# Columns of a gather table, two per VectorE operation

## The chip, the cores and the metric

The kernel runs on one core of a Trainium2 chip. The metric is the device time of one execution in microseconds (us). The engines in the text are PE (TensorE, with its weight loads as PEld), DVE (VectorE), ACT (ScalarE), POOL (GpSimd) and SP (SyncE), which here only issues DMAs.

## The reference

One layer of a graph network in float32. There are 12,500 nodes with 48 features, 400,000 edges with 32 features, and a hidden width of 128. The edges are sorted by destination.

```python
h = jnp.maximum(_layernorm(x, axis=-1), 0.0)
x_i, x_j = h[dst], h[src]
hid = relu(concatenate([x_i, x_j, edge_attr], axis=1) @ W1 + b1)
msg = hid @ W2 + b2
out = x + segment_sum(msg, dst, num_segments=12500)
```

The product with W1 can be parted: one part depends on the destination node, one on the source node and one on the edge. So two tables over the nodes hold the first two parts, and W2 is applied after the sum over the edges of a node.

## The kernel before, in words

A first stage (up to 67 us) computes the layer norm and builds two tables in DRAM with one row of 128 values per node: `tab_a` (the destination's part, with b1) and `tab_b` (the source's part).

The second stage, `windows`, goes over the edges in 391 chunks of 1024 edges, 8 tiles of 128. Since the edges are sorted, the destinations of a chunk lie in a window of `W` = 80 nodes, so a small one-hot matrix can stand for the gather by destination and for the sum. The source rows are in no order. They are the work that the change is about, and reach PE's sum in three ways:

- **gathers**: POOL issues one indirect DMA per tile (L358), which brings 128 rows of `tab_b` into the buffer `gb`. It has six buffers.
- **rows**: SP issues 12 DMAs of single rows per chunk (`rows`, L292); 128 of them, from several chunks, make a tile `gs` that replaces one gather. 36 tiles are made so.
- **columns**: the first 13 chunks (`BUILD`) also load `tab_b` and transpose it into SBUF, into `bt` (128 x 12,500: one column per node). From then on DVE and ACT copy single columns out of `bt` by an address in a register into a tile `gt` (`columns`, L339). PE transposes the tile and adds it to `pre` (`turned`, L394). `PARTS` says which columns of each chunk are whose: DVE 27 and 17, ACT 28 and 32. These 104 columns per chunk (`PART`) make 305 tiles that need no gather. The list `BYCOLS` names the chunk of each tile. 377 chunks copy columns.

The addresses stand in a table `last`; `load` (L274) brings the numbers of one part from it into an engine's registers with one instruction (TENSOR_LOAD).

The order on every engine is written out by hand (`tc.manual_schedule()`). In iteration c of the loop:

1. `prepare(c)`: SP loads the window's rows of `tab_a` (`rhs`, L347), the edge features (`lhs`, L349) and the destinations (`row`, L351). POOL issues the gathers of chunk c: eight, less one if the chunk has a tile of columns and one if it has a tile of rows. DVE compares the destinations with the window's first node (L366, one-hot in `lhs`, its sum in `deg`), loads the numbers of part 1, and makes the transposed one-hot `hot` (L372).
2. DVE's columns of parts 0 and 1.
3. PE: `before(c-1)` (L384, one-hot and edge features times `rhs` into `pre`), `fold(c-2)` (L416 and L419, the sum over the edges into `p_g`), `turned(c-1)` (L394).
4. ACT's columns of part 2; then `hidden(c-1)`: DVE adds `pre` and `gb` (L403, and L405 for a tile of rows), ACT applies the relu (L407 for a tile of columns, L408 for the rest).
5. ACT's columns of part 3; `add(c-2)`: DVE adds `p_g` to the window's place in a running buffer `seg` (L426). Every 12 chunks a finished segment of 1024 nodes is multiplied by W2, added to x and stored (L452 to L458), and the running buffer is changed (L442 to L444).
6. The numbers of parts 0 and 2 of chunk c+1 are loaded.

POOL's gathers of a chunk wait for a free `gb`, which `hidden` of an earlier chunk gives back. POOL also clears the three `deg` tiles (L251) at the start of `windows`.

Of the kernel before, what the change touches and what calls it, by code (L numbers as in the profile page):

```python
# [8 lines left out]
F32 = mybir.dt.float32  # L9
I32 = mybir.dt.int32  # L10
AF = mybir.ActivationFunctionType
ALU = mybir.AluOpType
# [4 lines left out]
P = 128  # L17
N, D, DE, HID, E = 12500, 48, 32, 128, 400000
# [6 lines left out]
NCH = (NT + T - 1) // T  # L25
W = 80
# [4 lines left out]
L = 1024  # L31
FAR = L - W
# [11 lines left out]
U8 = mybir.dt.uint8  # L44
# [5 lines left out]
COLS = BUILD + 1  # L50
ROWS0 = 3
END = NT // T

PARTS = ((True, 0, 27, 1), (True, 27, 17, 28), (False, 44, 28, 48), (False, 72, 32, 76))
PART = sum(n for _, _, n, _ in PARTS)
BASE = 108
RPART = 12

BT0 = 16512


SEG, NEXT, SEG2 = 122, 123, 124
WIDTH = 128
SLOTS = (NCH + 2 + P - 1) // P
MOST = 32

# [137 lines left out]
def windows(nc, tc, gp, bt, ident, idx, x_t, tab_a, tab_b, dst, edge_t, w1, w2s, b2s, out_t):  # L204


    srci, rel, bw, wrow, last = idx
    with ExitStack() as es:
        one = es.enter_context(tc.tile_pool(name="wone", bufs=1))
        ld = es.enter_context(tc.tile_pool(name="ld", bufs=3))  # L210
        gtp = es.enter_context(tc.tile_pool(name="gtp", bufs=3))
# [5 lines left out]
        ps_w = es.enter_context(tc.tile_pool(name="ps_w", bufs=1, space=PSUM))  # L217


        wnum = ps_w.tile([P, W], F32, name="wnum")  # L220
        nc.vector.tensor_scalar_add(wnum, wrow, -HALF)


        bt8 = bt.bitcast(U8)
        for _, _, n, at in PARTS:
            nc.vector.tensor_scalar(
                last[:, :, at : at + n], last[:, :, at : at + n], 4, BT0,
                op0=ALU.mult, op1=ALU.add,
            )
        rows_at = slice(BASE + 1, BASE + 1 + RPART)  # L230
# [3 lines left out]
        tab8 = tab_b.rearrange("n h -> (n h)").bitcast(U8)  # L234
# [8 lines left out]
        segs = []  # L243
        for k in range(2):
            seg = one.tile([P, 2, L], F32, name=f"seg{k}")
            nc.vector.memset(seg, 0.0)
            segs.append(seg)
        degs = []
        for k in range(3):
            deg = one.tile([W, P], F32, name=f"deg{k}")  # L250
            nc.gpsimd.memset(deg, 0.0)  # L251
            degs.append(deg)

        rhss = []
        for k in range(3):
            rhs = one.tile([P, HID], F32, name=f"rhs{k}")
            nc.sync.dma_start(rhs[W:K, :], w1[2 * D :, :])
            rhss.append(rhs)
        st = {}
        gts = {}  # L260
        gss = {}

        def group(c):

            return divmod(c + OFF, GQ)
# [15 lines left out]
        def node(n):  # L281
            return n.with_bounds(min_val=0, max_val=N - 1)
# [32 lines left out]
        regs = {}  # L315

        def load(c, part):

            dve, first, n, at = PARTS[part]
            n = max(0, min(n, len(BYCOLS) * P - ((c - COLS) * PART + first))) if c >= COLS else 0  # L320
            engine = mybir.EngineType.DVE if dve else mybir.EngineType.Activation
            if part == 0 and 2 <= c < NCH + 2:
                base, *nodes = numbers(c, at - 1, n + 1, engine)
                st[c - 2]["base"] = base.with_bounds(min_val=0, max_val=FAR)
            else:
                nodes = numbers(c, at, n, engine) if n else []
            regs[c, part] = nodes

        def columns(c, part):

            dve, first, _, _ = PARTS[part]
            copy = nc.vector.tensor_copy if dve else nc.scalar.copy
            for k, at in enumerate(regs.pop((c, part), [])):
                j, e = divmod((c - COLS) * PART + first + k, P)
                of = BYCOLS[j]
                if of not in gts:
                    gts[of] = gtp.tile([HID, P], F32, name="gt")
                at = at.with_bounds(min_val=BT0, max_val=BT0 + 4 * (N - 1)) - BT0
                copy(gts[of].bitcast(U8)[:, 4 * e : 4 * e + 4], bt8[:, bass.ds(at, 4)])  # L339

        def prepare(c):
            n = min(T, NT - c * T)
            at = c * CE
            m = max(0, min(RPART, len(BYROWS) * P - (c - ROWS0) * RPART)) if c >= ROWS0 else 0
            base, *nodes = numbers(c, BASE, 1 + m, mybir.EngineType.SP)
            rhs = rhss[c % 3]
            nc.sync.dma_start(rhs[:W, :], tab_a[bass.ds(node(base), W), :])  # L347
            lhs = ld.tile([P, CE], F32, name="lhs")
            nc.sync.dma_start(lhs[W:K, : n * P], edge_t[:, at : at + n * P])  # L349
            row = ld.tile([W, CE], I16, name="row")  # L350
            nc.sync.dma_start(  # L351
                row[:, : n * P],
                dst[at : at + n * P].rearrange("(o e) -> o e", o=1).to_broadcast([W, n * P]),
            )
            st[c] = dict(n=n, rows=nodes)
            gb = gp.tile([P, T, HID], F32, name="gb")
            for t in range(n - (c in BYCOLS) - (c in BYROWS)):
                nc.gpsimd.indirect_dma_start(  # L358
                    out=gb[:, t, :], out_offset=None, in_=tab_b[:, :],
                    in_offset=bass.IndirectOffsetOnAxis(  # L360
                        ap=srci[:, c * T + t : c * T + t + 1], axis=0
                    ),
                )

            deg = degs[c % 3]
            nc.vector.tensor_scalar(  # L366
                lhs[:W, : n * P], row[:, : n * P], bw[:, c : c + 1], None,
                op0=ALU.is_equal, op1=ALU.add, accum_out=deg[:, :1],
            )
            load(c, 1)  # L370
            hot = wp.tile([P, T, W], F32, name="hot")
            nc.vector.tensor_tensor(  # L372
                hot[:, :n, :], wnum.unsqueeze(1).to_broadcast([P, n, W]),
                rel[:, c * T : c * T + n].unsqueeze(2).to_broadcast([P, n, W]), op=ALU.is_equal,
            )
            st[c].update(rhs=rhs, lhs=lhs, gb=gb, deg=deg, hot=hot)

        def before(c):
# [43 lines left out]
        def add(c):  # L422

            s = st.pop(c)
            to = segs[group(c)[0] % 2][:, :, bass.ds(s["base"], W)]
            nc.vector.tensor_add(to, to, s["p_g"])  # L426

        xs = {}
# [31 lines left out]
        with tc.manual_schedule():  # L460
            for c in range(NCH + 2):
                if c < NCH:
                    prepare(c)
                    if c < BUILD:
                        part = turn_load(c)
                    rows(c, st[c].pop("rows"))
                columns(c, 0)
                columns(c, 1)
                if 0 <= c - 1 < NCH:
                    before(c - 1)  # L470
                if 0 <= c - 2 < NCH:
# [157 lines left out]
def tile_gnn_preln(  # L629
# [129 lines left out]
    outside = nc.values_load(flag[:1, :1], min_val=0, max_val=1)  # L759

    with tc.If(outside == 0) as cmp:
        windows(nc, tc, gp, bt, ident, (srci, rel, bw, wrow, last), x_t, tab_a, tab_b, dst16, edge_t,
                w1, w2s, b2s, out_t)
    with cmp.Else():
        general(nc, tc, bt, ident, x_t, tab_a, tab_b, src_it, dst_it, dst, edge_t, w1, w2s, b2s,
# [71 lines left out]
```

## Time and profile before

| | |
|---|---|
| median of 3 runs | 4946.85 us (4942.31 to 4949.29) |
| the profiled execution | 4948.09 us, span 4946.4 us |
| granted PE clock, mean | 0.607 |
| instructions | 92158 |
| DMA | 363.63 MB, mean 74 GB/s |
| POOL idle before a gather, released by DVE's L426 | 1273.1 us in 337 times |

The span is the time from the first to the last instruction of the profiled execution; the time beside it has what lies around it. The busy shares are means over the whole span. The seven or eight gathers of a chunk are called a burst. A line such as `gt<-bt 128x4 uint8 x16540 | 1516.0, 193 | 1464.2 <-issue 1457.9` says: 16540 operations that write `gt` from `bt`, 1516.0 us busy in all, 193 ns each, 1464.2 us of idle time of the engine just before them, of which 1457.9 us ended with "issue" (the engine waited for nothing that the profile shows). Operations overlap, so 193 ns is the time from the start of one to its end, not the distance to the next.

### The profile page before, as it was taken

To read this page: it belongs to the slowest core of one execution; us is meant where nothing else is said; L and a number is where in the kernel's file an instruction comes from. 1 tells how busy PE (TensorE), PEld (TensorE's weight loads), DVE (VectorE), ACT (ScalarE), POOL (GpSimd) and SP (SyncE) were. 2 spreads that over 40 slices of the span, in tenths; PEclk is the share of its full clock that TensorE was granted. 3 is DMA by queue.
4 is the path that set the end of the run, shared out by engine and by line. 5 is a ranking of instruction groups with operands and counts; after the bars stand their busy time and mean duration, and the time that the engine had idled before them with its cause. 6 is when DMAs were issued, how large, how long until landed. Compare 5 with 4: busy or idle time off the path is not lost. (4 is left out here: it accounts for less than half of the span.)

```text
span 4946.4 us, 92158 instructions
## 1 busy us (share of the span) xinstructions
PE 3197.2 (65%) x14504; PEld 2884.0 (58%) x14504; DVE 2942.6 (59%) x18764; ACT 2864.2 (58%) x23270; POOL 2675.9 (54%) x2812
## 2 busy tenths in 40 slices
PE   4565666666666666666666666666666666666666
PEld 3555556555555555656555555655666555555656
DVE  3255666666666666566666666666566666666665
ACT  2146666666566666566656566666566666566665
POOL 5555555555555555555555555555555555555552
PEclk7665655566666565556565666555555665666555
DMA  5422222222222222222222222222222222222221
GB/s 208 111 78 71 70 70 67 68 70 72 70 70 68 67 70 71 70 70 69 66 70 71 70 70 68 67 70 70 70 70 68 68 69 71 70 69 69 70 67 51
DMA packets 214695, 363.63 MB, mean 74 GB/s; under 512 B 70419, under 2 KB 119717, under 8 KB 212805
## 3 DMA queue, kind: packets, MB, share of 16 engines
q0 software_dynamic: 89120, 182.66, 14.4%
q1 hardware_dynamic: 124704, 174.89, 11.8%
q14 instruction: 491, 4.01, 0.3%
q8 instruction: 120, 1.97, 0.2%
q10 hardware_dynamic: 260, 0.10, 0.0%
HBM read 337.91 MB, written 22.07 MB: 73 GB/s over the span
## 5 line engine op out<-in xcount | busy, mean ns | idle before, releaser
L358 POOL DMA_INDIRECT gb<-tab_b,srci x2784 | 2654.2, 953 | 2167.6 <-DVE seg L426 1273.1
L339 ACT COPY gt<-bt 128x4 uint8 x22500 | 2421.0, 189 | 1761.1 <-issue 1734.7
L339 DVE COPY gt<-bt 128x4 uint8 x16540 | 1516.0, 193 | 1464.2 <-issue 1457.9
L416 PE MATMUL p_g<-hot,hid 128*128 128x80 f32 x6250 | 1368.2, 407 | 1557.6 <-ACT hid L408 1446.3
L416 PEld LDWEIGHTS p_g<-hot,hid 128*128 128x128 f32 x6250 | 1291.5, 314 | 1648.2 <-ACT hid L408 1528.5
L384 PEld LDWEIGHTS pre<-rhs,lhs 112*128 112x128 f32 x6250 | 1254.8, 306 | 140.1 <-issue 95.7
L384 PE MATMUL pre<-rhs,lhs 112*128 112x128 f32 x6250 | 1291.4, 393 | 52.1 <-DVE hid L403 38.8
L366 DVE TENSOR_SCALAR_CACHE_REDUCE lhs<-row,bw 80x1024 f32<-80x1024 int16 x391 | 498.1, 1274 | 253.5 <-issue 181.1
L403 DVE TENSOR_TENSOR hid<-pre,gb 128x896 f32<-128x896 f32 (+2 forms) x391 | 429.7, 1099 | 67.5 <-remote 53.8
L408 ACT ACTIVATE hid<-hid 128x896 f32<-128x896 f32 (+1 forms) x391 | 376.1, 962 | 120.4 <-DVE hid L403 91.1
L372 DVE TENSOR_TENSOR hot<-wnum,rel 128x640 f32<-128x640 f32 x391 | 322.0, 823 | 95.7 <-issue 95.7
L394 PE MATMUL pre<-ident,gt 128*128 128x128 f32 x610 | 220.0, 464 | 93.6 <-remote 49.8
L419 PE MATMUL p_g<-ident,deg 80*128 80x80 f32 x782 | 237.4, 405 | 2.7 <-issue 2.7
L394 PEld LDWEIGHTS pre<-ident,gt 128*128 128x128 f32 x610 | 164.0, 328 | 101.3 <-remote 53.6
L419 PEld LDWEIGHTS p_g<-ident,deg 80*128 80x128 f32 x782 | 203.4, 317 | 2.7 <-issue 2.7
L426 DVE TENSOR_TENSOR seg<-seg,p_g 128x160 f32 x391 | 120.9, 309 | 51.3 <-issue 23.4
L452 PE MATMUL p_f<-seg,w2s 128*48 128x512 f32 (+1 forms) x134 | 121.9, 1010 | 0.4 <-DVE seg L426 0.4
L407 ACT ACTIVATE hid<-pre 128x128 f32<-128x128 f32 x305 | 81.9, 268 | 60.8 <-DVE hid L403 51.7
L453 PE MATMUL p_f<-seg,b2s 1*48 1x512 f32 (+1 forms) x134 | 111.2, 924 | 0.0
L453 PEld LDWEIGHTS p_f<-seg,b2s 1*48 1x48 f32 x134 | 14.5, 159 | 102.0 <-issue 102.0
L311 ACT COPY bt<-pre 128x1024 f32<-128x1024 f32 (+1 forms) x13 | 12.4, 957 | 94.7 <-remote 71.5
L454 DVE TENSOR_TENSOR xseg<-xseg,p_f 48x512 f32<-48x512 f32 (+1 forms) x67 | 45.0, 671 | 29.7 <-PE p_f L453 22.5
(65 smaller groups left out, 348.7 us busy)
## 6 DMA issues: line engine op xcount, KB each, us to landing
gs<-tab_b SPq DMA_DIRECT2D x4608, 0.5 KB
row<-in_dst SPq DMA_DIRECT2D x390, 160.0 KB
lhs<-in_edge_t SPq DMA_DIRECT2D x390, 128.0 KB
gb<-tab_b,srci POOLq DMA_INDIRECT x2784
rhs<-tab_a SPq DMA_DIRECT2D x391, 40.0 KB
xseg<-in_x_t SPq DMA_DIRECT2D x33, 192.0 KB
out_x<-xseg SPq DMA_DIRECT2D x33, 192.0 KB
hid<-tab_b SPq DMA_DIRECT2D x12, 512.0 KB
```

The lines of the kernel that those rows point to most:

```text
L339: copy(gts[of].bitcast(U8)[:, 4 * e : 4 * e + 4], bt8[:, bass.ds(at, 4)])
L358: nc.gpsimd.indirect_dma_start(out=gb[:, t, :], out_offset=None, in_=tab_b[:, :], in_offset=bass.IndirectOffsetOnAxis(ap=srci[:, c * T + t ...
L366: nc.vector.tensor_scalar(lhs[:W, : n * P], row[:, : n * P], bw[:, c : c + 1], None, op0=ALU.is_equal, op1=ALU.add, accum_out=deg[:, :1],)
L372: nc.vector.tensor_tensor(hot[:, :n, :], wnum.unsqueeze(1).to_broadcast([P, n, W]), rel[:, c * T : c * T + n].unsqueeze(2).to_broadcast([P ...
L384: nc.tensor.matmul(pre[:, t, :], s["lhs"][:K, t * P : (t + 1) * P], s["rhs"][:K, :], start=True, stop=c not in BYCOLS or t < n - 1,)
L394: nc.tensor.matmul(s["pre"][:, s["n"] - 1, :], gts.pop(c), ident, start=False, stop=True)
L403: nc.vector.tensor_add(h[:, :g, :], pre[:, :g, :], s["gb"][:, :g, :])
L408: nc.scalar.activation(h[:, :m, :], h[:, :m, :], AF.Relu)
L416: nc.tensor.matmul(p_g[:, 0, :], s["h"][:, t, :], s["hot"][:, t, :], start=t == 0, stop=t == n - 1)
L419: nc.tensor.matmul(p_g[:, 1, :], s["deg"], ident[:W, :W], start=True, stop=True)
L452: nc.tensor.matmul(p_f[:, :n], w2s, seg[:, 0, s], start=True, stop=False)
L453: nc.tensor.matmul(p_f[:, :n], b2s[:1, :], seg[:1, 1, s], start=False, stop=True)
```

## The change

- DVE no longer copies single columns. One `tensor_scalar` takes two: its input is a pair of words, all ones and zero (`first`, in PSUM beside `wnum`), its two scalars are two columns of `bt` at register addresses, and the two operations are AND and XOR on bits. The first word becomes colA XOR colB, the second colB. When a group of pairs is done, one `tensor_tensor` (`part_pairs`) XORs the second words into the first, and so leaves colA and colB.
- ACT copies one float32 instead of four bytes.
- DVE's columns come in three parts, 24, 18 and 12 (54 for 44), each loaded by an instruction of its own; ACT's stay 28 and 32 (60). `PART` becomes 114, so 334 tiles instead of 305 come from columns, and POOL issues 2755 gathers instead of 2784.
- On DVE, part 0 moves ahead of `hot`; its load for the next chunk comes straight after `hidden`, ahead of part 2's parting and of `add`.
- The place of `add` and the row address of `rhs` come out of the table `last` as byte addresses, without a register instruction for each; `seg` gets a pool of its own and `last` wider rows (136 for 128).
- The `deg` tiles are made and cleared ahead of the first stage.

In the new file the pair operation is L361, the parting L375, ACT's copy L368, POOL's gather L400, the one-hots L408 and L415, `hidden` L447, ACT's relu of the eight or seven tiles L451, `turned` L438 and `add` L475.

```diff
-PARTS = ((True, 0, 27, 1), (True, 27, 17, 28), (False, 44, 28, 48), (False, 72, 32, 76))
+PARTS = (
+    (True, 0, 24, 1), (True, 24, 18, 25), (True, 42, 12, 43),
+    (False, 54, 28, 56), (False, 82, 32, 84),
+)
...
+        segs = [seg.tile([P, 2, L], F32, name=f"seg{k}") for k in range(2)]
...
-        wnum = ps_w.tile([P, W], F32, name="wnum")
+        wmask = ps_w.tile([P, W + 2], F32, name="wnum")
+        wnum = wmask[:, :W]
         nc.vector.tensor_scalar_add(wnum, wrow, -HALF)
+
+        first = wmask[:, W:].bitcast(I32)
+        nc.vector.memset(first[:, :1], -1)
+        nc.vector.memset(first[:, 1:], 0)
...
             if part == 0 and 2 <= c < NCH + 2:
                 base, *nodes = numbers(c, at - 1, n + 1, engine)
-                st[c - 2]["base"] = base.with_bounds(min_val=0, max_val=FAR)
+                st[c - 2]["base"] = base
...
         def columns(c, part):
-            dve, first, _, _ = PARTS[part]
-            copy = nc.vector.tensor_copy if dve else nc.scalar.copy
-            for k, at in enumerate(regs.pop((c, part), [])):
-                j, e = divmod((c - COLS) * PART + first + k, P)
+            dve, first_of, _, _ = PARTS[part]
+            nodes = regs.pop((c, part), [])
+            step = 2 if dve else 1
+            runs = {}
+            for k in range(0, len(nodes), step):
+                j, e = divmod((c - COLS) * PART + first_of + k, P)
                 of = BYCOLS[j]
                 if of not in gts:
                     gts[of] = gtp.tile([HID, P], F32, name="gt")
-                at = at.with_bounds(min_val=BT0, max_val=BT0 + 4 * (N - 1)) - BT0
-                copy(gts[of].bitcast(U8)[:, 4 * e : 4 * e + 4], bt8[:, bass.ds(at, 4)])
+                if dve:
+                    nc.vector.tensor_scalar(
+                        gts[of].bitcast(I32)[:, e : e + 2], first,
+                        column(nodes[k]).bitcast(I32), column(nodes[k + 1]).bitcast(I32),
+                        op0=ALU.bitwise_and, op1=ALU.bitwise_xor,
+                    )
+                    runs.setdefault(of, [e, e])[1] = e + 2
+                else:
+                    nc.scalar.copy(gts[of][:, e : e + 1], column(nodes[k]).bitcast(F32))
+            odd[c, part] = [(gts[of], *run) for of, run in runs.items()]
+
+        def part_pairs(c, part):
+            for gt, e0, e1 in odd.pop((c, part), []):
+                two = gt.bitcast(I32)[:, e0:e1].rearrange("h (k t) -> h k t", t=2)
+                nc.vector.tensor_tensor(
+                    two[:, :, 0], two[:, :, 0], two[:, :, 1], op=ALU.bitwise_xor
+                )
...
         def prepare(c):
...
-            nc.sync.dma_start(rhs[:W, :], tab_a[bass.ds(node(base), W), :])
+            base = base.with_bounds(min_val=0, max_val=4 * HID * (N - 1))
+            nc.sync.dma_start(
+                rhs.bitcast(U8)[:W, :],
+                taba8[bass.ds(base, 4 * HID * W)].rearrange("(w h) -> w h", w=W),
+            )
...
             load(c, 1)
+            columns(c, 0)
             hot = wp.tile([P, T, W], F32, name="hot")
...
+            load(c, 2)
...
         def add(c):
-            to = segs[group(c)[0] % 2][:, :, bass.ds(s["base"], W)]
+            k = group(c)[0] % 2
+            of = SEG0 + k * SEG_SIZE
+            at = s["base"].with_bounds(
+                min_val=of, max_val=of + 4 * FAR, guaranteed_mod_val=0, out_of_modulus=4
+            ) - of
+            to = segs[k].bitcast(U8)[:, :, bass.ds(at, 4 * W)].bitcast(F32)
             nc.vector.tensor_add(to, to, s["p_g"])
...
-                columns(c, 0)
+                if c >= NCH:
+                    columns(c, 0)
                 columns(c, 1)
+                part_pairs(c, 0)
+                columns(c, 2)
+                part_pairs(c, 1)
...
-                columns(c, 2)
+                columns(c, 3)
                 if 0 <= c - 1 < NCH:
                     hidden(c - 1)
-                load(c, 3)
-                columns(c, 3)
+                load(c + 1, 0)
+                part_pairs(c, 2)
+                load(c, 4)
+                columns(c, 4)
                 if 0 <= c - 2 < NCH:
                     add(c - 2)
...
-                load(c + 1, 0)
-                load(c + 1, 2)
+                load(c + 1, 3)
...
+    degs = []
+    for k in range(3):
+        deg = const.tile([W, P], F32, name=f"deg{k}")
+        nc.gpsimd.memset(deg, 0.0)
+        degs.append(deg)
     gp = ctx.enter_context(tc.tile_pool(name="gp", bufs=6))
```

More of the change, by code (lines that the diff above doesn't have):

```diff
@@ L52 @@
 END = NT // T
-PARTS = ((True, 0, 27, 1), (True, 27, 17, 28), (False, 44, 28, 48), (False, 72, 32, 76))
+PARTS = (
+    (True, 0, 24, 1), (True, 24, 18, 25), (True, 42, 12, 43),
+    (False, 54, 28, 56), (False, 82, 32, 84),
+)
 PART = sum(n for _, _, n, _ in PARTS)
-BASE = 108
+BASE = 116
 RPART = 12
 BT0 = 16512
-SEG, NEXT, SEG2 = 122, 123, 124
-WIDTH = 128
+SEG0 = 123360
+SEG_SIZE = 8 * L
+SEG, NEXT, SEG2 = 130, 131, 132
+PLACE0 = 133
+WIDTH = 136
 SLOTS = (NCH + 2 + P - 1) // P
@@ L204, in windows @@
 def windows(nc, tc, gp, bt, ident, idx, x_t, tab_a, tab_b, dst, edge_t, w1, w2s, b2s, out_t):
-    srci, rel, bw, wrow, last = idx
+    srci, rel, bw, wrow, last, degs = idx
     with ExitStack() as es:
+        seg = es.enter_context(tc.tile_pool(name="segs", bufs=1))
+        segs = [seg.tile([P, 2, L], F32, name=f"seg{k}") for k in range(2)]
         one = es.enter_context(tc.tile_pool(name="wone", bufs=1))
@@ L229, in windows @@
             )
-        rows_at = slice(BASE + 1, BASE + 1 + RPART)
+        rows_at = slice(BASE, BASE + 1 + RPART)
         nc.vector.tensor_scalar(
@@ L233, in windows @@
         )
-        tab8 = tab_b.rearrange("n h -> (n h)").bitcast(U8)
+        tab8, taba8 = (t.rearrange("n h -> (n h)").bitcast(U8) for t in (tab_b, tab_a))
         place = PARTS[0][3] - 1
@@ L241, in windows @@
             )
-        segs = []
-        for k in range(2):
-            seg = one.tile([P, 2, L], F32, name=f"seg{k}")
-            nc.vector.memset(seg, 0.0)
[L247 to L252, printed above, removed]
+        at_place = slice(place, place + 1)
+        nc.vector.scalar_tensor_tensor(
+            last[:, :, at_place], last[:, :, at_place], 4.0, last[:, :, PLACE0 : PLACE0 + 1],
+            op0=ALU.mult, op1=ALU.add,
+        )
+        for seg in segs:
+            nc.vector.memset(seg, 0.0)
         rhss = []
@@ L327, in load, with column @@
             regs[c, part] = nodes
-        def columns(c, part):
-            dve, first, _, _ = PARTS[part]
-            copy = nc.vector.tensor_copy if dve else nc.scalar.copy
-            for k, at in enumerate(regs.pop((c, part), [])):
-                j, e = divmod((c - COLS) * PART + first + k, P)
+        def column(at):
+            at = at.with_bounds(
+                min_val=BT0, max_val=BT0 + 4 * (N - 1), guaranteed_mod_val=0, out_of_modulus=4
+            ) - BT0
+            return bt8[:, bass.ds(at, 4)]
+        odd = {}
+        def columns(c, part):
+            dve, first_of, _, _ = PARTS[part]
[4 more added lines that the diff above has]
+                j, e = divmod((c - COLS) * PART + first_of + k, P)
                 of = BYCOLS[j]
@@ L346, in prepare @@
             rhs = rhss[c % 3]
-            nc.sync.dma_start(rhs[:W, :], tab_a[bass.ds(node(base), W), :])
+            base = base.with_bounds(min_val=0, max_val=4 * HID * (N - 1))
+            nc.sync.dma_start(
+                rhs.bitcast(U8)[:W, :],
+                taba8[bass.ds(base, 4 * HID * W)].rearrange("(w h) -> w h", w=W),
+            )
             lhs = ld.tile([P, CE], F32, name="lhs")
@@ L761, in tile_gnn_preln @@
     with tc.If(outside == 0) as cmp:
-        windows(nc, tc, gp, bt, ident, (srci, rel, bw, wrow, last), x_t, tab_a, tab_b, dst16, edge_t,
+        windows(nc, tc, gp, bt, ident, (srci, rel, bw, wrow, last, degs), x_t, tab_a, tab_b, dst16, edge_t,
                 w1, w2s, b2s, out_t)
@@ L790 @@
     numbers[2 : NCH + 2, SEG2] = seg
+    numbers[2 : NCH + 2, PLACE0] = SEG0 + of % 2 * SEG_SIZE
     numbers[:NCH, BASE] = first
```

## The prediction

> **What bounds the kernel now.** I read the busy shares first, then the costliest groups, the waits, and last the timeline of one chunk, because the shares alone name nobody.
>
> ```profile
> span 4946.4 us, 92158 instructions
> PE 3197.2 (65%) x14504; PEld 2884.0 (58%) x14504; DVE 2942.6 (59%) x18764; ACT 2864.2 (58%) x23270; POOL 2675.9 (54%) x2812
> L358 POOL DMA_INDIRECT gb<-tab_b,srci x2784 | 2654.2, 953 | 2167.6 <-DVE seg L426 1273.1
> L339 ACT COPY gt<-bt 128x4 uint8 x22500 | 2421.0, 189 | 1761.1 <-issue 1734.7
> L339 DVE COPY gt<-bt 128x4 uint8 x16540 | 1516.0, 193 | 1464.2 <-issue 1457.9
> ```
>
> No engine is over 65% busy. PE's idle time is a wait for ACT's relu and is not the cause. DVE and ACT are idle 1457.9 and 1734.7 us in front of column copies, released by "issue", that is by nothing the profile shows; over 377 chunks with columns that is 3.9 and 4.6 us per chunk. The timeline of a 7-gather chunk shows where (start, length, work, idle time before it in brackets):
>
> ```profile
> 2500.16 0.95 POOL L358 DMA_INDIRECT gb<-tab_b,srci  x1 [3.78 <-DVE seg L426]
> 2507.66 0.95 POOL L358 DMA_INDIRECT gb<-tab_b,srci  x1 [0.30 <-issue]
> 2512.30 0.95 POOL L358 DMA_INDIRECT gb<-tab_b,srci  x1 [3.69 <-DVE seg L426]
> ```
> ```profile
> 2500.61 1.27 DVE L366 TENSOR_SCALAR_CACHE_REDUCE lhs<-row,bw 80x1024 f32<-80x1024 int16 x1 [0.49 <-issue]
> 2502.12 0.82 DVE L372 TENSOR_TENSOR hot<-wnum,rel 128x640 f32<-128x640 f32 x1 [0.23 <-issue]
> 2502.86 2.01 DVE L339 COPY gt<-bt 128x4 uint8 x25
> 2505.81 0.31 DVE L339 COPY gt<-bt 128x4 uint8 x2 [0.93 <-issue]
> ...
> 2509.40 0.17 DVE L339 COPY gt<-bt 128x4 uint8 x1 [0.49 <-issue]
> 2510.09 0.95 DVE L339 COPY gt<-bt 128x4 uint8 x12 [0.52 <-issue]
> 2510.95 1.08 DVE L403 TENSOR_TENSOR hid<-pre,gb 128x896 f32<-128x896 f32 x1
> 2511.95 0.31 DVE L426 TENSOR_TENSOR seg<-seg,p_g 128x160 f32 x1
> ```
> ```profile
> 2505.82 0.19 ACT L339 COPY gt<-bt 128x4 uint8 x1 [0.51 <-issue]
> 2510.08 2.76 ACT L339 COPY gt<-bt 128x4 uint8 x28 [1.12 <-issue]
> 2512.92 0.94 ACT L408 ACTIVATE hid<-hid 128x896 f32<-128x896 f32 x1
> ```
>
> A burst of seven gathers begins at S = 2500.16, the next at 2512.30: period 12.14 us (the mean over chunks 30 to 380 is 12.34, with 8-gather and segment chunks). From about S+4.6 to S+9.9 DVE and ACT start one or two instructions per 0.7 us; outside they start copies 71 ns (DVE, 0.95 us for 12 with the tail) and 95.5 ns (ACT) apart. I call this the slow stretch. It falls with the gathers (the last ends at S+8.45) and ends on all engines together. So the loop is a ring: burst, slow stretch, the rest of DVE's columns, L403, and 1.35 us after L403's start the next burst, because L403 frees the gb buffer. (The profile names L426, which merely ended nearest.) DVE's part of the ring is 9.92 (S to 2510.08) + 0.87 (12 copies) + 1.35 = 12.14.
>
> ACT is nearly as full: 60 copies x 95.5 ns = 5.73, L407 and L408 about 1.35 with the gap, and 5.93 us of slow stretch that does 10 copies (worth 0.95): 12.06 us.
>
> **The change, part by part.** All against the profiled execution (4948.09 us, span 4946.4); the median shown is 4946.85, 0.03% lower.
>
> *Fewer gathers.* 114 instead of 104 columns per chunk give 334 tiles for 305: 29 gathers fewer (2755). A chunk with eight gathers takes 13 to 14 us against 12.1; the gather spacing of 1.25 us is the upper end, 0.95 the lower. I take 1.05: -30 us. 29 more transposing matmuls on PE cost nothing, since its slack before the next L403 in the chunk above is some 4 us; without it they would cost 29 x 0.71 = 21 us.
>
> *Columns on DVE.* Per chunk 44 copies go; 27 pair operations and 3 partings (a part or two per tile) come, 12 pairs of them ahead of L372. In the slow stretch DVE does about 8 instructions either way, now two columns each. What one pair operation costs is the main unknown: no instruction here has two pointer scalars or so few elements with one. Lower end: 71 ns, the start-to-start time of a copy. One scalar: L754 (391 elements, one pointer scalar) takes 419 ns; of this 204 is two elements per cycle, leaving 215, where L226 without a pointer (108 elements, 206 ns) leaves 150: +65. L366 start to its accumulator read is 1.207 us for 1024 elements, 1.067 + 0.140, where L372 (640 elements, 0.741) leaves 0.074: +66. So 71 + 66 = 137 ns if both scalars are fetched together, and 71 + 2 x 66 = 203 if one after the other. I take 137, the row with a pointer scalar measured start to start.
>
> "Perfetto Trace Analysis", Optimizing Scalar/DVE Operations, speaks against the form: about 60 ns for a DVE operation on SBUF but 125 on PSUM, and `first` lies in PSUM. L403 reads PSUM: 1.001 us to L426's start, 0.933 for its 896 elements and 0.068 left. The trace does not agree; by the page a pair would cost at least 125 ns and the forecast would hardly move.
>
> *Register loads.* DVE's 27 + 17 columns and the base were loaded by two instructions (28 numbers 1.86 us, 17 numbers 1.38, some 0.044 each and 0.63 fixed); now 25, 18 and 12: 1.73 + 1.42 + 1.16 = 4.31 against 3.24. The 18 stand between L366's successor (L408) and the first 12 pairs, the 12 behind L372's successor (L415), the 25 between hidden and part 2, add and the next L408. Behind that last one, add and the one-hot wait; the next burst does not, as it is released by hidden. L366 also started 1.80 us after L403 behind a load of 28 numbers, so its successor starts at much the same time (S+0.45). The first pair then starts between S+1.5 (load done under pairs still queued) and S+1.95 (1.42 after L408 was issued), and at S+1.25 if there is no wait at all; I take S+1.6.
>
> *The ring after.* p is the time of a pair. S+1.6, 12 pairs, L415 0.74: up to S+4.6 there are 4.6 - 1.6 - 0.74 = 2.26 us for pairs. Of 27 pairs and two partings, 8 fall in the slow stretch; what remains is 21p - 2.26. Period = 9.92 + 21p - 2.26 + 1.35 = 9.01 + 21p. With p = 0.137: 11.89 us. Level with 12.14 at p = 0.149. The bounds of the first pair move this by -0.35 and +0.35 us.
>
> *Columns on ACT.* Still 60; four bytes become one element. L408 (896) against L407 (128) gives 0.87 ns per element: -2.6 ns per copy, at most 0.16 us per chunk, none at least. ACT's period is 12.06 - 0.13 (50 copies outside the slow stretch) = 11.93, or 12.06 without it. I take 12.0, so ACT, not DVE, sets the period at p = 0.137: 12.14 - 12.0 = 0.14, x 377 = -53 us.
>
> *The rest.* The deg memsets move ahead of the node stage: the first gather waited until 67.24 behind memsets at 66.25 that waited 35.5 us for the node stage. It can now go when tab_b is written, perhaps at 49. But gathers slow the engines, and the copies that build tab_a run until 66. Between -18 and +10; I take -5. The register instructions before L426 and rhs (391 each, 69 ns) go; DVE's alone lies on the ring's side branch: 0 to -27 us, taken as 0, as it is behind hidden. SP's loads per chunk do not change.
>
> Sum: 4948 - 30 - 53 - 5 = 4860 us.
>
> **The rivals.**
> *Cheap pairs.* If scalars are fetched under the operation before, p = 0.075 to 0.11 and DVE is through its columns when the slow stretch ends. Then ACT lags until L407 and L408, which are single instructions worth 11 copies, start within the slow stretch; PE's 4 us of slack allow some of that. Period 11.4 to 11.8, -130 to -280 us, with -35: 4640 to 4790. For it: DVE's copies overlap their 193 ns down to 71. Against it: L366's +66 is a start-to-start time.
>
> *Dear pairs (slower).* The two scalars are fetched in series, p about 0.16 to 0.2. DVE's columns then outlast the slow stretch by more than the 12 copies did; L403's successor L447 and the next burst come later. At 0.17 the period is 12.58 (+0.44, +166 us, less 35: 5080), at 0.2 it is 13.21 (5315; 5185 with the first pair at S+1.25). It decides from p = 0.153, where the loss equals the 35 us saved. For it: the fetch of one scalar is not hidden in L366. Against it: nothing shows that a second adds to it.
>
> *Loads in front.* p is 0.137, but the load of 18 always holds the first pair until S+1.95: period 12.24, +38 - 35 = +3, about 4950. That is the case where the change does nothing: its two-columns gain is spent on 1.07 us more of register loads. For it: L372 now starts 0.23 us late behind such a load.
>
> **How the numbers follow.** A measurement can tell about 0.2%, 10 us, from no change. Chances: forecast 0.42, cheap pairs 0.18, dear pairs 0.28, loads in front 0.12. Faster: 0.37 of the forecast's 0.42 (the rest is split between same and slower, should ACT's form and DVE's slack give nothing), 0.18, and 0.03 of the last: 0.58. Same: 0.02 + 0.05 = 0.07. Slower: 0.03 + 0.28 + 0.04 = 0.35. The range runs from 4690, in the middle of the cheap case (0.07 below it), to 5085, p = 0.17 (0.13 above it). The forecast's own range is 4800 to 4930.
>
> **What would show it.** In the profile after: 2755 gathers; groups of 10126 pair operations at L361 and 22500 copies at L368 of one element. Pair to pair within a run gives p directly: 137 ns is my step, 75 or 200 the rivals. First pair to burst start gives 1.6. POOL's burst still follows hidden's (L447) start by 1.35 us. If ACT sets the period, DVE waits for work ahead of L447 or its idle time before pairs grows, and ACT's copies run without a wait for DVE. The start shows the first gather near 49 us. I am wrong if the slow stretch changes its length or place (as when DVE does more or fewer than 8 instructions in it), if ACT's copies become dearer, or if SP (some 10.8 us of 12.3 per chunk) becomes the bound.

## The result and the profile after

| | us |
|---|---|
| before, same chip | 4945.22 median of 4 (4942.31 to 4949.29) |
| after | 4981.66 median of 4 (4980.82 to 4988.03) |
| ratio | 1.0076, 95% interval 1.0058 to 1.0093 |
| profiled execution of after | 4980.82, span 4979.1 |

The kernel became 0.8% slower; 4860 was predicted. The page of the kernel after, the engines and the groups that answer to those shown of before:

```profile
span 4979.1 us, 86617 instructions
PE 3257.7 (65%) x14562; PEld 2939.7 (59%) x14562; DVE 3487.1 (70%) x13620; ACT 2818.9 (57%) x23299; POOL 2639.4 (53%) x2783
L400 POOL DMA_INDIRECT gb<-tab_b,srci x2755 | 2617.7, 950 | 2263.4 <-DVE hid L447 1022.0
L368 ACT COPY gt<-bt 128x1 f32 x22500 | 2366.5, 187 | 1760.0 <-issue 1740.8
L361 DVE TENSOR_SCALAR gt<-wnum,bt 128x2 int32<-128x2 int32 x10126 | 1999.8, 271 | 1129.6 <-issue 1096.9
```

The 29 gathers are gone (2755) and 10126 pair operations take 20252 columns, where 16540 copies took as many columns. DVE is busier (70%), yet it is still idle 1096.9 us with "issue" in front of its columns. ACT's idle time is what it was. The timeline of one chunk (the burst's first gather, DVE, then ACT) shows that the idle time has moved:

```profile
2497.52 0.95 POOL L400 DMA_INDIRECT gb<-tab_b,srci  x1 [3.71 <-DVE hid L447]
...
2497.94 1.27 DVE L408 TENSOR_SCALAR_CACHE_REDUCE lhs<-row,bw 80x1024 f32<-80x1024 int16 x1
2499.13 0.08 DVE L408 DVE_READ_ACCUMULATOR lhs<-row,bw 80x1 f32 x1
2501.88 2.35 DVE L361 TENSOR_SCALAR gt<-wnum,bt 128x2 int32<-128x2 int32 x12 [2.67 <-issue]
2504.14 0.82 DVE L415 TENSOR_TENSOR hot<-wnum,rel 128x640 f32<-128x640 f32 x1
2505.17 1.78 DVE L361 TENSOR_SCALAR gt<-wnum,bt 128x2 int32<-128x2 int32 x9 [0.21 <-issue]
...
2506.95 1.21 DVE L361 TENSOR_SCALAR gt<-wnum,bt 128x2 int32<-128x2 int32 x6
...
2508.82 1.09 DVE L447 TENSOR_TENSOR hid<-pre,gb 128x896 f32<-128x896 f32 x1 [0.59 <-issue]
...
2503.15 0.19 ACT L368 COPY gt<-bt 128x1 f32 x1 [1.00 <-issue]
2503.86 0.19 ACT L368 COPY gt<-bt 128x1 f32 x1 [0.52 <-issue]
...
2508.84 2.23 ACT L368 COPY gt<-bt 128x1 f32 x23 [0.51 <-issue]
```

Before, 25 copies ran at once and, until the slow stretch ended, the rest came one or two at a time. Now the pairs run in whole groups (12, 9, 6), even between 2503 and 2508.8, where ACT in the same chunk still starts one or two copies per 0.7 us. The hole lies ahead of the first pair: 2.67 us, and the pair starts 4.36 us after the burst. What fills it is a register load, which no row counts as busy. The single records of the trace have, in this chunk, DVE's three loads at 2497.744 (18 numbers, 4.042 us), 2502.353 (12 numbers, 2.723) and 2507.536 (25 numbers, 1.854); the next 18 follow at 2509.636. So DVE's queue goes around in 11.89 us, 8.62 of it in loads.

### The profile page after: what moved, and what is told of

The parts are those of the page before. It is cut to its first block, busy times and chain, and to the rows that moved or that the text cites. A ratio compares the mean times of both kernels' runs of the same rounds, so it can differ in the third digit from the quotient of the medians.

```text
span 4979.1 us, 86617 instructions
## 1 busy us (share of the span) xinstructions
PE 3257.7 (65%) x14562; PEld 2939.7 (59%) x14562; DVE 3487.1 (70%) x13620; ACT 2818.9 (57%) x23299; POOL 2639.4 (53%) x2783
## 4 chain that ended last, share of the span: by engine, by line
DVE 23%; issue 20%; POOL 7%; ACT 7%; DVEq 5%; PE 3%; DMA 1%; ACTq 1%; another core or an unknown queue 0%; SPq 0%; POOLq 0%
DVE gt L361 14%; POOL gb L400 7%; ACT gt L368 6%; DVEq L284 4%; DVE hid L447 3%; DVE hot L415 2%; PE p_g L460 1%; DMA gb<-tab_b,srci 1%; PE pre L428 1%; DVE gt L375 1%; ACTq L284 1%; DVE lhs L408 1%; ACT hid L452 1%; DVE seg L475 1%; DVE xseg L503 0%
## 5 line engine op out<-in xcount | busy, mean ns | idle before, releaser
L400 POOL DMA_INDIRECT gb<-tab_b,srci x2755 | 2617.7, 950 | 2263.4 <-DVE hid L447 1022.0
L368 ACT COPY gt<-bt 128x1 f32 x22500 | 2366.5, 187 | 1760.0 <-issue 1740.8
L361 DVE TENSOR_SCALAR gt<-wnum,bt 128x2 int32<-128x2 int32 x10126 | 1999.8, 271 | 1129.6 <-issue 1096.9
L460 PE MATMUL p_g<-hot,hid 128*128 128x80 f32 x6250 | 1388.3, 412 | 1532.1 <-ACT hid L452 1134.3
L460 PEld LDWEIGHTS p_g<-hot,hid 128*128 128x128 f32 x6250 | 1310.6, 318 | 1621.3 <-ACT hid L452 1203.3
L428 PEld LDWEIGHTS pre<-rhs,lhs 112*128 112x128 f32 x6250 | 1270.8, 310 | 99.4 <-issue 88.7
L408 DVE TENSOR_SCALAR_CACHE_REDUCE lhs<-row,bw 80x1024 f32<-80x1024 int16 x391 | 495.5, 1267 | 65.5 <-DMA row<-in_dst 59.8
L447 DVE TENSOR_TENSOR hid<-pre,gb 128x896 f32<-128x896 f32 (+2 forms) x391 | 425.8, 1089 | 33.8 <-issue 18.1
L415 DVE TENSOR_TENSOR hot<-wnum,rel 128x640 f32<-128x640 f32 x391 | 318.0, 813 | 0.0
L438 PE MATMUL pre<-ident,gt 128*128 128x128 f32 x668 | 239.2, 461 | 87.5 <-remote 71.2
L375 DVE TENSOR_TENSOR gt<-gt 128x12 int32<-128x12 int32 (+7 forms) x1266 | 192.6, 161 | 104.8 <-DVE hid L447 70.0
L438 PEld LDWEIGHTS pre<-ident,gt 128*128 128x128 f32 x668 | 179.3, 328 | 94.3 <-remote 76.1
L451 ACT ACTIVATE hid<-pre 128x128 f32<-128x128 f32 x334 | 90.3, 270 | 123.2 <-DVE hid L447 64.8
L475 DVE TENSOR_TENSOR seg<-seg,p_g 128x160 f32 x391 | 122.6, 314 | 41.5 <-remote 26.3
```

The costliest lines, as they stand in the source:

```text
L361: nc.vector.tensor_scalar(gts[of].bitcast(I32)[:, e : e + 2], first, column(nodes[k]).bitcast(I32), column(nodes[k + 1]).bitcast(I32), op0 ...
L368: nc.scalar.copy(gts[of][:, e : e + 1], column(nodes[k]).bitcast(F32))
L400: nc.gpsimd.indirect_dma_start(out=gb[:, t, :], out_offset=None, in_=tab_b[:, :], in_offset=bass.IndirectOffsetOnAxis(ap=srci[:, c * T + t ...
L408: nc.vector.tensor_scalar(lhs[:W, : n * P], row[:, : n * P], bw[:, c : c + 1], None, op0=ALU.is_equal, op1=ALU.add, accum_out=deg[:, :1],)
L415: nc.vector.tensor_tensor(hot[:, :n, :], wnum.unsqueeze(1).to_broadcast([P, n, W]), rel[:, c * T : c * T + n].unsqueeze(2).to_broadcast([P ...
L428: nc.tensor.matmul(pre[:, t, :], s["lhs"][:K, t * P : (t + 1) * P], s["rhs"][:K, :], start=True, stop=c not in BYCOLS or t < n - 1,)
```

## The experiments

Each kernel ran beside runs of before on the same chip. The chips were of two kinds, which only the later runs showed. On the first kind before took 4945 to 5003 us, and the traces have the slow stretch. On the second it took 3575 to 3582 us, and the traces are without it (before itself was timed there but has no trace): not one of 19501 steps from one DVE copy to the next is over 0.4 us in e8_again, where e8_third, the same program on a chip of the first kind, has 2158. Ratios are therefore always to before on the same chip, and kernels are compared only on chips of one kind.

### Where the numbers stand

In the table `last`, parts 1 and 2 of the change begin at words 25 and 43. All long loads of before, and the change's other long loads, begin at a multiple of four words. e1_fours moves the parts:

```diff
-    (True, 0, 24, 1), (True, 24, 18, 25), (True, 42, 12, 43),
-    (False, 54, 28, 56), (False, 82, 32, 84),
+    (True, 0, 24, 1), (True, 24, 18, 28), (True, 42, 12, 48),
+    (False, 54, 28, 60), (False, 82, 32, 88),
...
-BASE = 116
+BASE = 120
...
-SEG, NEXT, SEG2 = 130, 131, 132
-PLACE0 = 133
+SEG, NEXT, SEG2 = 133, 134, 135
+PLACE0 = 26
```

> After with one edit: in the table of numbers each part begins at a place that is a multiple of four words (parts 1 and 2 at 28 and 48 for 25 and 43). Theory (place): the loads of 18 and 12 numbers take 4.1 and 2.8 us because they begin at an odd word; they fall to about 1.4 and 1.15 us, DVE's idle time ahead of the first pair (2.4 to 2.7 us in a chunk) falls below 1 us, and ACT's 11.9 us become the period: 4780 to 4880 us. Rival (position): the loads are slow because of where they stand among register-addressed operations, or of how many registers are live: they stay at 4.1 and 2.8 us and the time stays at 4980.

e2_twos puts them at words 26 and 46:

> As e1_fours, but parts 1 and 2 begin at places 26 and 46, even and not multiples of four. If an even word is enough, the loads take 1.4 and 1.15 us and the time is that of e1_fours; if it takes a multiple of four, they take 4.1 and 2.8 us and the time stays at 4980.

e3_before_odd does the reverse to before: `(True, 27, 17, 28)` becomes `(True, 27, 17, 29)`.

> Before with one edit: part 1's 17 numbers begin at place 29 instead of 28. Theory (place): that load takes 0.235 x 17 = about 4.0 us instead of 1.38, and L372 and the copies start 2.6 us later in each chunk; if the slow stretch then also holds the copies back as it did, 25 of them fall behind it: up to +1.8 us a chunk, 5000 to 5600 us. Rival (position): 1.38 us and 4946 us as before.

Measured against before on the same chip (5003.1 us): e1_fours 4853.33 us, 0.9693 (0.9673 to 0.9713); e2_twos 5005.3 us in one run; e3_before_odd 5132.29 us, 1.0255 (1.0238 to 1.0272). So e1_fours is 3% below e2_twos, whose loads are as long as those of after. The lists of DVE's loads (shortest, median, longest, in ns) of after, e1_fours, e2_twos and e3_before_odd:

```profile
L284 DVEq TENSOR_LOAD <-last x1174: 306/2799/5044, 139.1 to 4966.1; - x196
```
```profile
L284 DVEq TENSOR_LOAD <-last x1174: 304/1604/2792, 141.4 to 4850.0; - x196
```
```profile
L284 DVEq TENSOR_LOAD <-last x1174: 304/2800/5023, 139.5 to 4990.5; - x196
```
```profile
L274 DVEq TENSOR_LOAD <-last x800: 306/1949/4322, 125.6 to 5118.3; - x160
```

In the first three the median is that of the middle size: the 12 in after and e2_twos, the 18 in e1_fours. By single records, the load of 18 takes 4.16 us in after and e2_twos and 1.60 in e1_fours, the load of 12 takes 2.80, 2.80 and 0.87, and the load of 25, always from word 0, takes 1.90 in all three. The 17 of before went from 1.38 us at word 28 to 3.94 at word 29. So a load from a place that is no multiple of four words costs about 0.23 us for each number, and an even word does not help. The position on the queue and the number of live registers are the same in after and e1_fours, so they do not make the difference; nor does the slow stretch, as after_again below has loads of 4.16 and 2.80 us without it.

Length has a part too. e9_60_54 (below) loads 16 and 20 numbers from multiples of four, in 1.12 and 1.38 us. So 20 numbers take less than the 18 of e1_fours (1.60) and as long as the 17 of before (1.38): the numbers left over after the whole groups of four cost 0.24 to 0.26 us each there as well (17 and 18 against 16).

With the loads mended, DVE's idle time is no longer ahead of its pairs (1096.9 us in after) but ahead of `hidden` (33.8 us in after). Of e1_fours:

```profile
L361 DVE TENSOR_SCALAR gt<-wnum,bt 128x2 int32<-128x2 int32 x10126 | 1999.8, 273 | 94.5 <-issue 84.6
L447 DVE TENSOR_TENSOR hid<-pre,gb 128x896 f32<-128x896 f32 (+2 forms) x391 | 428.0, 1095 | 575.0 <-issue 223.3
```

So something else sets the time. The chain of work that ended last, in shares of the span, of after and of e1_fours:

```profile
DVE 23%; issue 20%; POOL 7%; ACT 7%; DVEq 5%; PE 3%; DMA 1%; ACTq 1%; another core or an unknown queue 0%; SPq 0%; POOLq 0%
```
```profile
ACT 51%; issue 34%; PE 5%; ACTq 3%; DVE 1%; DVEq 1%; another core or an unknown queue 0%; SPq 0%; DMA 0%
```

In e1_fours DVE has left the chain and ACT with its own held-up copies ("issue") is on it. The median period, from `hidden` to `hidden` over chunks 30 to 380, is 11.66 us for 12.33 in e2_twos on the same chip.

### The same kernel without the slow stretch

after_again is the changed kernel on a chip of the second kind, with e1_again (e1_fours), e8_again and e9_again beside it.

> The changed kernel once more, so that it stands beside the next three on one chip. Before took 4945 and 5003 us on the chips of the first runs and 3576 us on that of e5_one to e9_66_48, whose trace has no slow stretch. On a chip with the slow stretch: 0.5 to 1% slower than before, as measured. On one without it, theory (place): DVE's own chain of loads and pairs (1.9 + 4.15 + 2.8 us of loads, 2.9 us of pairs and partings behind the last one, 0.4 of waits) holds the period at about 12.2 us still, 4600 to 4900 us and thus some 30% slower than before there. Rival (the slow stretch makes it slow): about as before, 3500 to 3700 us.

It took 4808.99 us where before took 3575.41: 1.3449 (1.3427 to 1.3472). The timeline of DVE there:

```profile
2499.98 2.34 DVE L361 TENSOR_SCALAR gt<-wnum,bt 128x2 int32<-128x2 int32 x12 [2.73 <-issue]
...
2506.28 1.08 DVE L447 TENSOR_TENSOR hid<-pre,gb 128x896 f32<-128x896 f32 x1
...
2511.86 1.40 DVE L361 TENSOR_SCALAR gt<-wnum,bt 128x2 int32<-128x2 int32 x7 [2.76 <-issue]
```

11.88 us from first pair to first pair, as DVE's queue took on the other chip (11.89). DVE's queue of loads holds the loop at this pace with and without the slow stretch. Where the slow stretch already made before slow, this costs 0.8%, and where not, 34%.

> e1_fours once more. With the slow stretch: 0.969 of before, as measured, and ACT sets the period. Without it DVE does (8.5 us of work and 0.7 of waits a chunk): 3550 to 3750 us, 0.99 to 1.05 of before.

e1_again: 3780.46 us, 1.0562 (1.0543 to 1.0582), a little beyond the bound, with DVE 91% busy. So on that kind of chip the mended kernel is slower than before. That it is the price of the pairs is shown by the next two sections (e5_one and e8_again).

### The price of a pair

e4_sbuf makes `first` a tile of SBUF (`first = one.tile([P, 2], I32, name="firsts")`). e5_one takes the second scalar and its XOR away, and so leaves the second column of each pair out:

```diff
-                        column(nodes[k]).bitcast(I32), column(nodes[k + 1]).bitcast(I32),
-                        op0=ALU.bitwise_and, op1=ALU.bitwise_xor,
+                        column(nodes[k]).bitcast(I32), None,
+                        op0=ALU.bitwise_and,
```

> e1_fours with the pair of words (all ones, zero) in SBUF instead of PSUM. Theory (two scalars): pair to pair stays at 0.188 us, 58 ns more than a copy for each pointer scalar, and the time is that of e1_fours within 0.3%. Rival (PSUM): part of the 0.188 is the read from PSUM; pair to pair falls to about 0.125 us.

> e1_fours with the second pointer scalar and its XOR left out of every pair operation (so the second columns are not taken and the result is not the reference's). Theory (a fetch for each scalar): pair to pair falls from 0.188 to 0.130 us, half of the 117 ns above a copy's 71. Rival (a fixed price for the form): it stays at 0.188. The time should hardly move (-0 to -0.5% against e1_fours), since ACT sets the period there.

Median start to start: 0.188 us in after and e1_fours, 0.191 with `first` in SBUF, 0.127 with one scalar. The second scalar costs 61 ns, and the PSUM read nothing. The Trainium skill, in "Perfetto Trace Analysis", Optimizing Scalar/DVE Operations, gives a DVE operation an overhead of about 125 ns on PSUM and 60 on SBUF; that difference does not show here. The times: e4_sbuf 0.9689 of before (0.9673 to 0.9706), as e1_fours; e5_one 3528.59 us in one run beside 3576.2, 0.987 of before. It ran on a chip of the second kind, so its forecast against e1_fours was not tested; against e1_again there (1.056) it is 6.6% lower. As a pair takes 0.188 us and two single copies of one float32 take 0.12 (e8_again: 0.061 each), the pair as such is the dearer form.

### What the pairs bring

e8_singles undoes the pairs in e1_fours and keeps the parts, loads and places:

```diff
-                    nc.vector.tensor_scalar(
-                        gts[of].bitcast(I32)[:, e : e + 2], first,
-                        column(nodes[k]).bitcast(I32), column(nodes[k + 1]).bitcast(I32),
-                        op0=ALU.bitwise_and, op1=ALU.bitwise_xor,
-                    )
-                    runs.setdefault(of, [e, e])[1] = e + 2
+                    nc.vector.tensor_copy(gts[of][:, e : e + 1], column(nodes[k]).bitcast(F32))
```

> e1_fours with the pairs undone: DVE copies its 54 columns one by one (one float32 each, 71 ns), in the same three parts, loads and places; no parting. Theory (stock: in the slow stretch an engine has some 25 to 30 instructions in hand and then gets one or two per 0.7 us): 24 copies before L415 use up the stock, most of the 30 behind it wait for the end of the slow stretch at S+9.9, the period is 12.5 to 13 us: 3 to 7% above e1_fours. Rival (a load in the slow stretch renews the stock, so three loads were all that was needed): DVE is done by S+8, time within 0.5% of e1_fours. If the pairs gained by their price, 27 x 0.188 + 0.3 = 5.4 us against 54 x 0.071 = 3.8, singles should be faster or equal.

> e8_singles once more, beside e1_again. Without the slow stretch it took 0.987 of before. With it, theory (stock): 24 copies ahead of L415 use up the 25 to 30 instructions in hand, most of the next 30 wait, period 12.5 to 13 us: 3 to 7% above e1_again. Rival (a load in the slow stretch renews the stock): within 0.5% of e1_again.

> e8_singles once more: the two pairs of calls with it fell on chips whose traces have no slow stretch, where it took 0.987 of before and e1 1.056. On a chip with the slow stretch (before near 4950 to 5000 us), theory (stock): most of the 30 copies behind the second load wait, 1.00 to 1.04 of before, that is 3 to 7% above e1_fours' 0.969. Rival (a load in the slow stretch renews the stock, so the pairs bring nothing): 0.965 to 0.975 of before.

e8_singles and e8_again fell on chips without the slow stretch: 0.9869 (0.9852 to 0.9885) and 0.9873 (0.9856 to 0.9889), 6.5% below e1_again: without the slow stretch the pairs cost time. e8_third fell on a chip with it: 5108.65 us, 1.0217 (1.02 to 1.0234), 5% above e1_fours: there they save time. So the sign depends on the kind of chip. DVE's timeline in e8_third:

```profile
2505.92 1.55 DVE L360 COPY gt<-bt 128x1 f32 x24 [0.30 <-issue]
2507.38 0.81 DVE L409 TENSOR_TENSOR hot<-wnum,rel 128x640 f32<-128x640 f32 x1
2508.11 0.75 DVE L360 COPY gt<-bt 128x1 f32 x11
2509.79 0.21 DVE L360 COPY gt<-bt 128x1 f32 x2 [0.93 <-issue]
2510.51 0.15 DVE L360 COPY gt<-bt 128x1 f32 x1 [0.51 <-issue]
```

24 copies and 11 more run freely, then the rest trickle, one or two per 0.7 us. Free runs as long as these 35 are rare: in the middle chunk of 311 it is 26 copies. DVE's idle "issue" time in front of its copies is 1634.8 us here and 99.7 us in e8_again, the same program. With S again the start of the burst, the free run ends at S+4.7 in e8_third and, after 26 copies, at S+4.7 in before too (middle chunk of 323). In e3_before_odd, whose long load ends only at S+4.5, it has 25 copies and ends at S+7.4 (middle chunk of 312), well inside the slow stretch. So the number of instructions fits, and the time since the burst began does not. The time since the load ended, 2.7 to 2.9 us in these three, does not either: in e1_fours the 27 pairs run freely until 6.1 us after it. This is what one would see if an engine lives in the slow stretch on a stock of instructions taken in while it waited, and gets one or two per 0.7 us after that. Pairs need half as many, and take so long each that the stock lasts. In e1_fours 25 of 9000 steps from pair to pair are over 0.4 us, in e8_third 2158 of 19501 from copy to copy. The stock fits all these runs, but it is an inference: no view shows it.

### Who sets the mended kernel's time

e9_60_54 moves six columns from ACT to DVE (`(True, 24, 20, 28), (True, 44, 16, 48), (False, 60, 26, 64), (False, 86, 28, 92)`), e9_66_48 twelve.

> e1_fours with six columns of a chunk moved from ACT to DVE (60 and 54; 114 in all as before). Theory (ACT sets the period in e1_fours): 6 x 93 ns = 0.56 us a chunk, less what then ends on DVE: -1.5 to -4% against e1_fours. Rival (DVE sets it): +3 x 0.188 = 0.56 us a chunk, +4%.

> As e9_60_54 with twelve columns moved (66 and 48). Theory: up to -1.1 us a chunk, but DVE's last pairs now end near S+9.6, and SP needs some 10.8 us a chunk: -2 to -6% against e1_fours. Rival (DVE sets it): +1.1 us a chunk, +8%.

> e9_60_54 (six columns of a chunk from ACT to DVE) once more, beside e1_again. Without the slow stretch it took 1.068 of before, with DVE 95% busy. With it, theory (ACT sets the period in e1): 1.5 to 4% below e1_again. Rival (DVE sets it): 4% above.

> e9_60_54 (e1_fours with six columns of a chunk moved from ACT to DVE) once more, for a chip with the slow stretch, where e1_fours was 0.969 of before and ACT had 51% of its chain of waits. Theory (ACT sets the period there): 0.93 to 0.96 of before. Rival (DVE sets it there too): 1.00 to 1.01. On a chip without the slow stretch it is 1.065 again.

> e9_66_48 (twelve columns moved) once more, for a chip with the slow stretch. Theory (ACT sets the period of e1_fours, DVE that of this one: 33 pairs and 1.13 us more than e1's 8.5 to 9.2 us of DVE work a chunk): 0.92 to 0.98 of before. Rival (DVE sets it from the start): 1.04. On a chip without the slow stretch it is 1.129 again.

All five fell on chips without the slow stretch: 60 and 54 took 1.0675, 1.0647 and 1.0634 of before, 66 and 48 took 1.1288 and 1.1256. There DVE sets the time (95% busy in both). Six columns, three pairs, cost 0.8% against e1_again and not the 4% that the rival expected; part of them fell into idle time, as DVE was 91% busy in e1_again. For the chips with the slow stretch the question stays open; that ACT sets the time of e1_fours rests on its chain alone.

### The start

e6_late clears three tiles on POOL at the start of `windows`, on memory that the node stage used, so that the first gather waits as in before.

> e1_fours with three small memsets on POOL at the start of the window stage, on memory that the node stage has used, so that the first gather waits for the node stage (near 67 us) as it did in before. Theory (early gathers slow the building of tab_a: its last copy was at 118 us in after and at 66 us in before): the first hidden comes near 125 us instead of 140, and 10 to 16 us are won, less what the chunks after it give back: 0 to -0.3% against e1_fours (0.969 of before with the slow stretch, 1.056 without). Rival (the early start is a gain): +0.2 to +0.4%.

It took 0.9703 of before (0.9687 to 0.9719) against e1_fours' 0.9693: not told apart. Both halves of the mechanism are there, however. In after the first gather came at 50.50 us, and the last copies of `tab_a` waited:

```profile
75.88 0.69 DVE L187 COPY tab<-p_n 128x512 f32<-128x512 f32 x1 [10.45 <-remote]
107.44 0.69 DVE L187 COPY tab<-p_n 128x512 f32<-128x512 f32 x1 [30.86 <-remote]
```

In e6_late the corresponding last copies were done by 66.7 us and the first hidden came at 125.3 us, against 142.3 in e1_fours (140.0 in after, 124.3 in before). The chunks after it take most of that back: at chunk 10 after is 2.0 us behind before. A first gather 17 us earlier is worth nothing that these runs can tell (0.1% between the two ratios).

### A mixture

e10_mixed copies part 0 singly and keeps the pairs in parts 1 and 2 (`step = 2 if dve and part else 1`).

> e1_fours with single copies (one float32 each) in part 0 of DVE's columns, ahead of the slow stretch, and pairs in parts 1 and 2 alone, so that 24 columns are taken at 61 ns each and 30 at 94, and 18 instructions stand where e8_singles has 30. Without the slow stretch: DVE's work falls by 12 x 0.188 - 24 x 0.061 = 0.8 us a chunk against e1_fours, to some 8.3 us, below the 8.8 of seven gathers: 0.985 to 1.01 of before (e1 1.056, e8 0.987). With the slow stretch, theory (stock): of the 18 instructions some 12 go at once and 6 at one or two per 0.7 us, DVE ends near S+8.5 as in e1_fours, and ACT sets the period: 0.965 to 0.985 of before. Rival (the 24 copies use up the stock and the pairs behind them wait for S+9.9): 1.00 to 1.03.

> e10_mixed once more, for a chip with the slow stretch (without it, it took 0.987 of before). Theory (the instructions in the slow stretch count): 0.965 to 0.985 of before. Rival (the 24 copies use up the stock and the pairs behind them wait for S+9.9): 1.00 to 1.03.

Both runs fell on chips without the slow stretch: 0.9867 (0.9851 to 0.9884) and 0.9856 (0.9829 to 0.9882), as fast as singles and 6.6% below e1_again. It is 1.3 to 1.4% faster than before there, where after was 34% slower; with the slow stretch it was not measured. For chips with the slow stretch e1_fours, at 0.969, is faster than before and after (e4_sbuf and e6_late are not told apart from it).

## Why the prediction was wrong

**The step that failed: register loads.** The sum took 0.044 us per number and 0.63 fixed from two loads, and made the three loads 1.73 + 1.42 + 1.16 = 4.31 us. They measured 1.90 + 4.16 + 2.80 = 8.86 us. The fit used loads that all begin at a multiple of four words, and the diff's places 25 and 43 were not looked at. That is 4.5 us a chunk on a queue whose turn is 11.9 us, so DVE's queue became the wait that set the period, a ring that the prediction did not have. From multiples of four (e1_fours) the same loads take 1.90 + 1.60 + 0.87 = 4.37 us. That this is so near 4.31 is luck, as the single terms miss by 0.17, 0.18 and -0.29. The first pair came at S+4.36 in the chunk shown (2501.88 against a burst from 2497.52), and at S+4.3 in the middle one of 302 chunks, far outside the bounds S+1.25 to S+1.95. The 2.76 us beyond the S+1.6 that was taken match the 2.74 us that the load of 18 took beyond its 1.42. The rival "loads in front" had this wait, but at S+1.95 and without the place as its reason. e1_fours, without that term, ran at 0.969 of before, a larger gain than the 0.982 that was forecast.

**The price of a pair** was 0.188 us, near the upper bound of 203 ns for two scalars in series, and not the 0.137 that was taken. By the formula this is the dear case, with a period of 9.01 + 21 x 0.188 = 12.96 us. e1_fours has this price and a median period of 11.66. So the price was misjudged and so was its weight: the rival "dear pairs" had the price right, but where the slow stretch is present it is refuted as a cause. Without the slow stretch the price decides (e1_again against e5_one and e8_again). "Cheap pairs" is refuted by the 0.188 itself.

**The slow stretch** was taken as eight instructions on DVE, whatever they are. That was wrong for pairs: of some 9000 steps from pair to pair in after one is over 0.4 us; in before 2195 of 16164 steps from copy to copy are. Fewer instructions are, by e8_third against e1_fours, the gain (5%), and it was larger than forecast.

**ACT's term and the ring** held up in part. Once the loads are mended, ACT is on the chain (51%), with its copies 93 ns apart for 95 before. That L447 releases the burst also held: in e1_fours POOL's largest wait is for L447.

**The gathers** went as said, 29 fewer. **The start** was taken as -5 us and is not told from 0; gathers did delay `tab_a`, by 50 us, more than the range of +10 allowed for that stage alone, but later chunks hide it.

**Where the 33 us are** (by the spans, 4979.1 against 4946.4): 3.5 by chunk 30, 19.2 in chunks 30 to 380 (mean period 12.395 for 12.340), 10.3 in the ten after that, where the gathers run out and before drops to 7 to 11 us a chunk while after mostly stays at 12, held by its loads.

## What to carry to other kernels

Place each block of numbers that is loaded into registers at a multiple of four words, give it a length of whole fours where that is free, and take the price of a load from one at the same kind of place, not by size alone. Where an engine idles with "issue" in its single records, look for register loads on its queue: they are not counted as busy. An edit that halves the number of instructions can win though each is dearer, as it did here on the chips where the engines were held to one or two instructions per 0.7 us; on the others it lost. So run such a change on more than one chip.

## What the runs showed of the hardware

A load of registers from a place that is no multiple of four words takes 0.23 us a number (18: 4.16 us, 17: 3.94, 12: 2.80), from a multiple of four 1.60, 1.38 and 0.87 us. There 20 numbers (1.38 us) take less than 18. The second pointer scalar on DVE adds 61 ns to the distance between operations (0.127 us with one, 0.188 with two), and a first input in PSUM adds nothing against SBUF (0.188 and 0.191). The same program took 5003 us on one chip and 3576 us on another; the slow stretch, in which DVE and ACT start one or two copies per 0.7 us (on DVE after a free run of some 25), was in the traces of the first kind alone. What makes it, and why it is missing on other chips, stays open.
